# Layer 1's subset tables looked up by one float32 product in place of two float32r parts

## The chip, the core and the metric

The kernel runs on one NeuronCore of a Trainium2 chip. The metric is device time in microseconds (us) of one execution; three timed runs are summed up by their median. Beside them stands one profiled execution, from which every duration is taken. Engines are named as in the profile: PE is TensorE's matmuls, PEld its weight loads, DVE VectorE, ACT ScalarE, POOL GpSimd, SP the queue that issues most transfers.

## What is computed

Four graph layers run one after the other on 16 graphs of 1024 nodes with 128 features each; each layer's output is added to its input and normalised. The change touches layer 1 alone:

```python
def _L1_gnn_ref(x, adj, W, b):
    W1, W2 = (W[:d], W[d:])
    p = jnp.einsum('bnd,do->bno', x, W1 - W2)
    q = jnp.einsum('bnd,do->bno', x, W2)
    pre = p[:, :, None, :] + q[:, None, :, :] + b
    h = jax.nn.relu(pre) * adj[..., None]
    return jnp.max(h, axis=2)
```

For each node this is the maximum of `q` over the node's neighbours, plus `p`, cut at zero. Layer 0 is attention over the adjacency, layer 2 a sum over neighbours and two dense products. Layer 3 first thins the adjacency row by row, which is a long serial chain, and then runs three graph convolutions with batch norms.

## The kernel before, in words

**Maximum by tables.** The 1024 possible neighbours of a graph are cut into groups of six (`GS`). For each group there is a table of 64 rows: entry s is the largest `q` among the neighbours whose bit is set in s. `tables_of` builds these tables on DVE with features on partitions (`sub`). Which subset a node has is counted on PE: `count` multiplies a constant of plus and minus ones (`lit`) with the adjacency (`AT`), ACT turns the result into a one-hot column (`hot`), and a product of table and one-hot column picks the right entry (`look_up`). Two groups stand in one step: one in the upper 64 partitions, the other in the lower 64. DVE then takes the running maximum (`best`) of the 2 x 512 results.

**Slots.** One step of twelve neighbours is a slot; a graph has 86 (`NP`), and all 16 graphs 1376. Each slot has two halves of 512 nodes. In each half the program issues: the look-up of slot s into a two-bank buffer `pg` (two such buffers); pieces of layers 0 and 2 and of layer 3's thinning that a planner finds due; the count for slot s + 2; and, on DVE, the maximum over `pg`. Every second slot `table` transposes the next two steps' tables from `sub` (two transposes into `pt`) and ACT copies them out. The order in this loop on PE, ACT, DVE and POOL is written out by the program (`tc.manual_schedule`). The planner's costs and due times are constants in the code and the change does not touch them. Layer 3's thinning runs mainly on POOL and DVE beside the slots, from the generator `dilation`. After the loop come the rest of that thinning and layer 3's convolutions (`edges`, `convolve`, `sage`, `second`, `summed`).

**How a table gets its precision before.** [...] So the table is split into a high and a low float32r part. `table` writes `high`, the table cast to float32r, by ACT. `low_part`, called in the first half of every odd slot, adds `-high` to the bank that still holds the table (a product with `less`, minus the identity) and ACT casts what is left to `low`. `look_up` then multiplies `high` and `low` with `hot`, which is float32r too, and adds them in PSUM:

```python
for k, part in enumerate(tables[s - at]):
    for a in range(2):
        rows = slice(64 * a, 64 * a + 64)
        nc.tensor.matmul(pg[:, a], part[rows, at * P:(at + 1) * P], hots[s][rows, halves[h]],
                         start=(k == 0), stop=(k == 1))
```

For each half that is four products of 64 x 128 by 64 x 512: upper rows high, lower rows high, upper rows low, lower rows low. `pm` and `pt` share two banks (tag "subset"), `pg` has four.

Lines that matter: L106 `less`, L746 `hot`, L748 and L749 the count, L760 and L763 the table, L768 and L770 the low part, L779 the look-up, L831 the maximum, L286 other float32 products of 512 columns (`product_of`), used here to read what a float32 product takes.

Of the kernel before, what the change touches and what calls it, by code (L numbers as in the profile page):

```python
# [29 lines left out]
F32 = mybir.dt.float32  # L30
F32R = mybir.dt.float32r
# [8 lines left out]
B, N, D, H2 = 16, 1024, 128, 256  # L40
P = 128
# [30 lines left out]
def tile_graph_layers(ctx: ExitStack, tc, a, out):  # L72
    nc = tc.nc
    x, adj, adjT = a["x"], a["adj"], a["adjT"]
    halves = (slice(0, 512), slice(512, 1024))

    consts = ctx.enter_context(tc.tile_pool(name="consts", bufs=1))
# [13 lines left out]
    ident = consts.tile([P, P], F32, name="ident")  # L91
# [10 lines left out]
    nc.vector.memset(mhalf, -0.5)  # L102
    lit = consts.tile([CH, PC, P], F8, name="lit")
    nc.gpsimd.dma_start(out=lit, in_=a["lit"])
    less = consts.tile([P, P], F32R, name="less")
    nc.vector.tensor_scalar_mul(less, ident, -1.0)  # L106
    one_less = consts.tile([P, 1], F32, name="one_less")
    nc.sync.dma_start(out=one_less, in_=a["one_less"])

# [126 lines left out]
    def layers_012():  # L236
# [7 lines left out]
        w2 = right.enter_context(tc.tile_pool(name="w2", bufs=1, side="right"))  # L244
# [206 lines left out]
        def tables_of(b):  # L451

            if b:
                yield ask("V", 0, urgent=True, after=("tables", b - 1))
            for g0 in range(0, NP, TG):
                n_g = 2 * min(TG, NP - g0)
                yield ask("V", 0.01, same=True, urgent=True, after=("q", b))
                made.append((b, g0))
                yield ask("V", 0.1, same=True, urgent=True, after=("used", *made[-3]) if len(made) > 2 else None)
                qg = qs[b].rearrange("o (g s) -> o g s", s=GS)  # L460
                subs[b, g0] = w2.tile([P, TG, P], F32, name="sub", bufs=2)
                sub = subs[b, g0].rearrange("o t (a s) -> o (t a) s", a=2)
                nc.vector.memset(sub[:, :n_g, 0:1], LOWEST)
                for k in range(GS):
                    n = 1 << k
                    yield ask("V", 0.06 + n * n_g / 960, same=(n < 8), urgent=True)
                    nc.vector.tensor_max(sub[:, :n_g, n:2 * n], sub[:, :n_g, 0:n],  # L467
                                         qg[:, 2 * g0:2 * g0 + n_g, k:k + 1].to_broadcast([P, n_g, n]))
                happened["sub", b, g0] = now
            happened["tables", b] = now  # L470
# [214 lines left out]
        def load_x(b):  # L685
            X[b] = apool.tile([P, T, D], F32, name="X", bufs=3)
            nc.sync.dma_start(out=X[b], in_=x[b].rearrange("(t p) d -> p t d", p=P))
# [5 lines left out]
        def load_columns(at):  # L693
            b, c = divmod(at, T + 1)
            if b < B:
                rows = min(CH, N - c * CH)
                t = AT[at] = apool.tile([CH, N], F8, name="AT", bufs=4)
                if rows < CH:
                    nc.gpsimd.memset(t, 0.0)
                nc.gpsimd.dma_start(out=t[:rows], in_=adjT[b, c * CH:c * CH + rows])  # L700

        An, AT, subs, qs, ps, values, exps, bests, hots, tables = ({} for _ in range(10))
# [8 lines left out]
        def start(stream, first=False):  # L711
            pending[stream] = [next(stream, None), -9]
            streams.insert(0 if first else len(streams), stream)
# [27 lines left out]
        def count(s, h):  # L741

            b, g = divmod(s, NP)
            c, r = divmod(g, PC)
            if h == 0:
                hots[s] = w2.tile([P, N], F32R, name="hot", bufs=3)  # L746
            pm = psum.tile([P, 512], F32, tag="subset", name="pm", bufs=2)
            nc.tensor.matmul(pm, lit[:, r, :], AT[b * (T + 1) + c][:, halves[h]], start=True, stop=True)  # L748
            nc.scalar.activation(hots[s][:, halves[h]], pm, AF.Relu, bias=one_less)  # L749

        def table(s):

            b, g = divmod(s, NP)
            g0 = g - g % TG
            assert ("sub", b, g0) in happened, (s, [(x.__name__, pending[x]) for x in streams], room)
            pt = psum.tile([P, 512], F32, tag="subset", name="pt", bufs=2)[:, :2 * P]
            if g + 2 - g0 == min(TG, NP - g0):
                happened["used", b, g0] = now
            for k in range(2):
                nc.tensor.matmul(pt[:, k * P:(k + 1) * P], subs[b, g0][:, g - g0 + k, :], ident, is_transpose=True,  # L760
                                 start=(k == 0), stop=(k == 1))
            high = w2.tile([P, 2 * P], F32R, name="high", bufs=2)
            nc.scalar.copy(high, pt)  # L763
            tables[s] = pt, high

        def low_part(s):
            pt, high = tables[s]
            nc.tensor.matmul(pt, less, high, start=False, stop=True, skip_group_check=True)  # L768
            low = w2.tile([P, 2 * P], F32R, name="low", bufs=2)
            nc.scalar.copy(low, pt)  # L770
            tables[s] = high, low

        def look_up(s, h, pg):

            at = s % 2
            for k, part in enumerate(tables[s - at]):
                for a in range(2):
                    rows = slice(64 * a, 64 * a + 64)
                    nc.tensor.matmul(pg[:, a], part[rows, at * P:(at + 1) * P], hots[s][rows, halves[h]],  # L779
                                     start=(k == 0), stop=(k == 1))  # L780

        def finish(b):

            if b:
                best = bests.pop(b - 1)
                nc.vector.tensor_max(best[:, 0], best[:, 0], best[:, 1])
                nc.vector.tensor_add(ps[b - 1], best[:, 0], ps[b - 1])
            if b < B:
                bests[b] = w4.tile([P, 2, N], F32, name="best")

        def slot(s, last):

            nonlocal now, due, wants_bank
            now = s
            b, g = divmod(s, NP)
            if s >= 0 and g == 0:
                finish(b)
                if b + 1 < B:
                    start(tables_of(b + 1), True)
                    load_x(b + 1)  # L800
                    start(attend(b + 1))
                    start(scores(b + 1))
                if b:
                    start(rest(b - 1))
            if s >= 0 and g % PC == 0:
                load_columns(b * (T + 1) + g // PC + 2)
            for h in range(2):
                now = s + 0.5 * h
                for e in ROOM:
                    room[e] = min(room[e] + ROOM[e] / 2, ROOM[e])  # L810
                if s >= 0:
                    pg = psum.tile([P, 2, 512], F32, tag="wide", name="pg", bufs=2)
                    look_up(s, h, pg)
                advance(("PE",))
                advance(("A", "V", "Pool"))
                if s >= 0 and due <= now and not (wants_bank and taken >= 2 and given.get(taken - 2, 1e9) > now):
                    after, cost, wants_bank = next(dilate, (B * NP, 0, False))
                    due += after
                    room["V"] -= cost
                if h == 0 and s % 2 and s + 1 < last:  # L820
                    low_part(s + 1)
                if s + 2 < last:
                    count(s + 2, h)
                    if h and s % 2 == 0:
                        table(s + 2)
                if s >= 0:
                    own = bests[b][:, :, halves[h]]
                    if g == 0:
                        nc.vector.tensor_copy(own, pg)
                    else:  # L830
                        nc.vector.tensor_max(own, own, pg)  # L831
            if s >= 0:
                hots.pop(s)
# [19 lines left out]
        with tc.manual_schedule(engines={mybir.EngineType.PE, mybir.EngineType.Activation, mybir.EngineType.DVE,  # L853
                                         mybir.EngineType.Pool}):
            for s in range(-2, B * NP):
                slot(s, B * NP)
            finish(B)
        assert not streams, streams
        last = rest(B - 1)
# [68 lines left out]
    def load_share(b):  # L928
        part = sb.tile([P, N], F32, name="share")
        nc.sync.dma_start(out=part, in_=share[b].partition_broadcast(P))  # L930
        return part
# [132 lines left out]
    with ExitStack() as es:  # L1064
        layers_012()
# [8 lines left out]
    for b in range(B):  # L1074
        x0 = sb.tile([P, T, D], F32, name="h", bufs=2)
        nc.sync.dma_start(out=x0, in_=x3[b])
        part = load_share(b)
# [3 lines left out]
        if b + 1 < B:  # L1081
            start = len(nc.cur_bb.bb.instructions)
# [16 lines left out]
    for b in range(B):  # L1099
        near = ep.tile([P, T, N], F8, name="near", bufs=2)  # L1100
        nc.sync.dma_start(out=near, in_=kept[b])
        part = load_share(b)
# [72 lines left out]
```

## Time and profile before

| | us |
|---|---|
| runs | 6573.1, 6579.31, 6581.36 |
| median | 6579.31 |
| span of the profiled execution | 6568.2 |
| slots, from the first to the last look-up | 131.3 to 5278.8 |

Over the whole span, busy time and instructions by engine, and the span in 40 slices (each digit a busy share in tenths, PEclk the granted clock of TensorE in tenths):

```profile
PE 5661.4 (86%) x27177; PEld 2873.0 (44%) x27306; DVE 5317.8 (81%) x8130; ACT 3780.8 (58%) x6665; POOL 3794.2 (58%) x11157
...
PE   6989898989898989899989898888888768877998
PEld 3434344444343444444444444444443335555654
DVE  3999899999899999999999999999998844444445
ACT  4656566666666666666666666666665533333755
POOL 2675767676767776767677776767676611110113
PEclk8989899999898989898989998999898878888999
```

The first 32 slices are the slots: PE and DVE both nearly full. The last eight are layer 3. The groups of the look-up and of the table, by line (busy us, mean ns of one, then idle time of the engine before them and who ended it):

```profile
L749 ACT ACTIVATE hot<-pm,one_less 128x512 fp32r<-128x512 f32 x2752 | 1882.1, 688 | 1118.0 <-PE pm L748 1107.3
L779 PE MATMUL pg<-hot,high 64*128 64x512 f32 x5504 | 1471.9, 532 | 468.0 <-DVE best L831 426.2
L779 PE MATMUL pg<-hot,low 64*128 64x512 f32 x5504 | 1166.7, 420 | 0.0
...
L770 ACT CAST low<-pt 128x256 fp32r<-128x256 f32 x688 | 255.5, 371 | 393.7 <-PE pt L768 389.3
...
L768 PE MATMUL pt<-high,less 128*128 128x256 f32 x688 | 300.9, 437 | 66.3 <-ACT high L763 58.7
L760 PE MATMUL pt<-ident,sub 128*128 128x128 f32 x1376 | 292.8, 297 | 24.5 <-ACT hot L749 22.0
```

[...] records overlap, and the sum of durations is above the time that the engine was held; a step from one start to the next tells more. "64*128 64x512" is a product whose weights have 64 rows and 128 columns and whose moving operand has 64 rows and 512 columns.

### The profile page before, as it was taken

How to read it: one execution, taken by the hardware profiler on the slowest of the kernel's cores; microseconds unless marked ns; L12 is line 12 of the kernel's file. 1: busy time of each engine (PE TensorE's matmuls, PEld its weight loads, DVE VectorE, ACT ScalarE, POOL GpSimd, SP SyncE). 2: the span in 40 equal slices, each digit the busy share in tenths (PEclk: the TensorE clock that was granted, in tenths of full speed). 3: DMA queues.
4: the chain of work that ended last, by engine and by line, in shares of the span. 5: the costliest groups of instructions: out<-in, count | busy, mean ns of one | idle time of the engine just before them, and what ended most of it. 6: DMA issues, size and time to landing. Idle time of an engine off the chain costs nothing. (4 is left out here: it accounts for less than half of the span.)

```text
span 6568.2 us, 85836 instructions
## 1 busy us (share of the span) xinstructions
PE 5661.4 (86%) x27177; PEld 2873.0 (44%) x27306; DVE 5317.8 (81%) x8130; ACT 3780.8 (58%) x6665; POOL 3794.2 (58%) x11157
## 2 busy tenths in 40 slices
PE   6989898989898989899989898888888768877998
PEld 3434344444343444444444444444443335555654
DVE  3999899999899999999999999999998844444445
ACT  4656566666666666666666666666665533333755
POOL 2675767676767776767677776767676611110113
PEclk8989899999898989898989998999898878888999
DMA  5121212121212121212121212121110056564555
GB/s 38 13 28 23 31 23 36 21 28 26 28 26 29 24 30 27 27 27 28 26 27 27 30 26 33 23 31 27 27 26 12 14 80 125 110 119 106 199 170 183
DMA packets 478380, 317.00 MB, mean 48 GB/s; under 512 B 301162, under 2 KB 429668, under 8 KB 473828
## 3 DMA queue, kind: packets, MB, share of 16 engines
q0 software_dynamic: 105648, 84.20, 14.9%
q1 hardware_dynamic: 367600, 226.13, 11.9%
q8 instruction: 213, 3.49, 0.2%
q10 hardware_dynamic: 4676, 1.19, 0.1%
q14 instruction: 243, 1.99, 0.1%
HBM read 412.71 MB, written 117.18 MB: 81 GB/s over the span
## 5 line engine op out<-in xcount | busy, mean ns | idle before, releaser
L831 DVE TENSOR_TENSOR best<-best,pg 128x1024 f32<-128x1024 f32 x2720 | 3234.4, 1211 | 298.4 <-PE pg L779 289.4
L749 ACT ACTIVATE hot<-pm,one_less 128x512 fp32r<-128x512 f32 x2752 | 1882.1, 688 | 1118.0 <-PE pm L748 1107.3
L779 PE MATMUL pg<-hot,high 64*128 64x512 f32 x5504 | 1471.9, 532 | 468.0 <-DVE best L831 426.2
L779 PE MATMUL pg<-hot,low 64*128 64x512 f32 x5504 | 1166.7, 420 | 0.0
L748 PE MATMUL pm<-AT,lit 120*128 120x512 fp8e4 x2752 | 1135.9, 413 | 17.9 <-ACT hot L749 10.1
L779 PEld LDWEIGHTS pg<-hot,high 64*128 64x128 f32 x5504 | 545.7, 195 | 1271.7 <-DVE best L831 801.5
L616 POOL TENSOR_SCALAR sc<-low_counts,half_mask,rest 16x1 f32<-16x1 f32 x992 | 426.5, 430 | 403.9 <-DVE rest L603 310.1
L779 PEld LDWEIGHTS pg<-hot,low 64*128 64x128 f32 x5504 | 570.2, 204 | 0.0
L748 PEld LDWEIGHTS <-lit 120*128 120x128 fp8e4 x2752 | 273.7, 99 | 618.7 <-issue 556.1
L621 POOL TENSOR_SCALAR sc<-sc 16x1 f32<-16x1 f32 x992 | 425.5, 429 | 105.0
L770 ACT CAST low<-pt 128x256 fp32r<-128x256 f32 x688 | 255.5, 371 | 393.7 <-PE pt L768 389.3
L618 POOL TENSOR_SCALAR sc<-sc 16x1 f32<-16x1 f32 x992 | 351.6, 354 | 107.7
L980 POOL TENSOR_TENSOR length<-length,mhalf 128x8 f32<-128x8 f32 x48 | 78.9, 1644 | 572.2 <-DVE length L979 572.2
L624 POOL TENSOR_SCALAR last_rank<-V,sc 16x31 f32<-16x31 bf16 (+30 forms) x992 | 384.7, 388 | 0.0
L623 POOL TENSOR_SCALAR hit<-V,sc 16x31 bf16<-16x31 bf16 (+30 forms) x992 | 372.7, 376 | 0.0
L768 PE MATMUL pt<-high,less 128*128 128x256 f32 x688 | 300.9, 437 | 66.3 <-ACT high L763 58.7
L467 DVE TENSOR_TENSOR sub<-sub,q 128x24 f32<-128x24 f32 (+11 forms) x768 | 306.5, 400 | 24.6 <-ACT q L289 10.5
L937 ACT CAST m<-near 128x1024 fp32r<-128x1024 fp8e4 x256 | 253.4, 1044 | 113.1 <-DVE near L906 59.4
L619 POOL TENSOR_SCALAR sc<-sc 16x1 f32<-16x1 f32 x992 | 269.9, 272 | 83.4
L760 PE MATMUL pt<-ident,sub 128*128 128x128 f32 x1376 | 292.8, 297 | 24.5 <-ACT hot L749 22.0
L626 POOL TENSOR_TENSOR low_counts<-low_counts,hit 16x31 f32<-16x31 f32 (+30 forms) x992 | 264.6, 267 | 77.7
L377 PE MATMUL pav<-v,eT 128*128 128x128 f32 x2048 | 307.6, 296 | 1.9 <-ACT eT L370 1.9
(258 smaller groups left out, 9431.7 us busy)
## 6 DMA issues: line engine op xcount, KB each, us to landing
removed<-gone SPq DMA_DIRECT2D x128, 256.0 KB
An<-in_adj_dram POOLq DMA_DIRECT2D x16, 1024.0 KB, 14.8
E<-in_adj_dram POOLq DMA_DIRECT2D x128, 128.0 KB, 6.8
gone_all<-removed POOLq DMA_DIRECT2D x64, 256.0 KB, 12.1
near<-in_adjT_dram POOLq DMA_DIRECT2D x16, 1024.0 KB, 17.3
kept<-near SPq DMA_DIRECT2D x16, 1024.0 KB
share<-share SPq DMA_DIRECT2D x32, 512.0 KB
hidden<-r SPq DMA_DIRECT2D x32, 512.0 KB
```

The lines of the kernel that those rows point to most:

```text
L377: nc.tensor.matmul(pav, eT[:, c, :], values[b][:, c, :], start=(c == 0), stop=(c == T - 1))
L467: nc.vector.tensor_max(sub[:, :n_g, n:2 * n], sub[:, :n_g, 0:n], qg[:, 2 * g0:2 * g0 + n_g, k:k + 1].to_broadcast([P, n_g, n]))
L616: gp.tensor_scalar(half, mine, half_mask[:, m], rest[:, n:n + 1], op0=ALU.mult, op1=ALU.add)
L618: gp.tensor_scalar(sf, half, 5.5, sf, op0=ALU.is_gt, op1=ALU.mult)
L621: gp.tensor_scalar(to, at, sf, none, op0=ALU.subtract, op1=ALU.subtract)
L623: gp.tensor_scalar(hit[:, n, n + 1:], V[:, n, n + 1:], at, None, op0=ALU.is_equal)
L624: gp.tensor_scalar(last[:, n + 1:], V[:, n, n + 1:], to, None, op0=ALU.is_le)
L748: nc.tensor.matmul(pm, lit[:, r, :], AT[b * (T + 1) + c][:, halves[h]], start=True, stop=True)
L749: nc.scalar.activation(hots[s][:, halves[h]], pm, AF.Relu, bias=one_less)
L768: nc.tensor.matmul(pt, less, high, start=False, stop=True, skip_group_check=True)
L779: nc.tensor.matmul(pg[:, a], part[rows, at * P:(at + 1) * P], hots[s][rows, halves[h]], start=(k == 0), stop=(k == 1))
L831: nc.vector.tensor_max(own, own, pg)
```

## The change

The table is no longer split. `table` copies it out of PSUM once, as float32; `low_part` and `less` are gone; `hot` is float32; and `look_up` makes one float32 product for each half of the rows:

```diff
-    less = consts.tile([P, P], F32R, name="less")
-    nc.vector.tensor_scalar_mul(less, ident, -1.0)
...
-                hots[s] = w2.tile([P, N], F32R, name="hot", bufs=3)
+                hots[s] = w2.tile([P, N], F32, name="hot", bufs=3)
...
-            high = w2.tile([P, 2 * P], F32R, name="high", bufs=2)
-            nc.scalar.copy(high, pt)
-            tables[s] = pt, high
-
-        def low_part(s):
-            pt, high = tables[s]
-            nc.tensor.matmul(pt, less, high, start=False, stop=True, skip_group_check=True)
-            low = w2.tile([P, 2 * P], F32R, name="low", bufs=2)
-            nc.scalar.copy(low, pt)
-            tables[s] = high, low
+            tables[s] = w2.tile([P, 2 * P], F32, name="table", bufs=2)
+            nc.scalar.copy(tables[s], pt)
...
-            for k, part in enumerate(tables[s - at]):
-                for a in range(2):
-                    rows = slice(64 * a, 64 * a + 64)
-                    nc.tensor.matmul(pg[:, a], part[rows, at * P:(at + 1) * P], hots[s][rows, halves[h]],
-                                     start=(k == 0), stop=(k == 1))
+            for a in range(2):
+                rows = slice(64 * a, 64 * a + 64)
+                nc.tensor.matmul(pg[:, a], tables[s - at][rows, at * P:(at + 1) * P], hots[s][rows, halves[h]],
+                                 start=True, stop=True)
...
-                if h == 0 and s % 2 and s + 1 < last:
-                    low_part(s + 1)
```

For each half of a slot there are two float32 products where there were four float32r products, and every second slot has one product and one ACT cast less.

## The prediction

> **What bounds the kernel now.** I read, in this order, the page's slices, the granted clock, the busy times of the slot loop, the groups by line, TensorE's own timeline in a dense stretch, and TensorE's waits. Busy times by stretch, the slot loop (first to last `pg` product) in the first line, columns busy microseconds of PE, PEld, DVE, ACT, POOL, then granted clock, DMA share and GB/s:
>
> ```profile
> 131.00:5279.00 5148.00, 4529.59 (x22015) 2168.15 (x22141) 4704.24 (x6944) 3168.41 (x5820) 3563.30 (x10742) 0.91 0.19 26
> ```
>
> The loop has 16 x 86 = 1376 slots: 5148 / 1376 = 3.741 us a slot, 78% of the span. DVE is busy for 91% of it (3.42 us a slot), PE for 88% (idle 618 us, 0.45 us a slot), ACT for 62%. Two engines are near their limit, DVE nearer. Who waits, TensorE's waits and then the groups:
>
> ```profile
> PE pg L779 <- DVE best L831: 426.2, 415, 12.8
> PE pt L768 <- ACT high L763: 57.9, 231, 1.6
> ...
> PE pg L779 <- DVE sub L463: 32.8, 37, 3.2
> ...
> L831 DVE TENSOR_TENSOR best<-best,pg 128x1024 f32<-128x1024 f32 x2720 | 3234.4, 1211 | 298.4 <-PE pg L779 289.4
> ```
>
> TensorE waits for DVE (426 us) more than DVE for TensorE (289 us): a balance leaning to DVE. How long a product really holds TensorE is not its duration but the step from its start to the next start. Timeline of PE, full clock (start, length, line, tile):
>
> ```profile
> 1991.18 0.39 PE L748 MATMUL pm<-AT,lit 120*128 120x512 fp8e4 x1
> 1991.51 0.50 PE L779 MATMUL pg<-hot,high 64*128 64x512 f32 x2
> 1991.84 0.40 PE L779 MATMUL pg<-hot,low 64*128 64x512 f32 x2
> 1992.17 1.13 PE L286 MATMUL pp<-xT,w_L_gnn_W 128*128 128x512 f32 x2
> 1993.13 0.38 PE L748 MATMUL pm<-AT,lit 120*128 120x512 fp8e4 x1
> ...
> 2008.30 0.39 PE L768 MATMUL pt<-high,less 128*128 128x256 f32 x1
> 2008.52 0.39 PE L748 MATMUL pm<-AT,lit 120*128 120x512 fp8e4 x1
> ```
>
> The reader is to see three things. The two 64-row look-ups of one part (x2) take 0.33 us together, not 0.33 each: single records start 3 ns apart, so the upper and lower 64 rows of the array run side by side. One half of a slot spends 0.33 us on `high` and 0.33 on `low`. And one true float32 product of 512 columns (`pp`) is two records and holds TensorE for 0.96 us: in single records the second starts 0.53 us after the first (0.105 of it a weight load that nothing covers, 0.428 the stream), and the next product 0.428 later. An engine view of what TensorE would need without waits: in 300 to 5100 us of the trace I replaced each step from start to start by the 20th percentile, at full clock, of steps between the same two kinds of product. The sum is 3831 of 4800 us: 2.985 us a slot. The rest of the 3.741 is 0.45 of waits and about 0.31 of half clock (the records grant half speed in 807 of those 4800 us).
>
> [...] a 512-column step is 0.217 to 0.227 us[...] and 2 x 0.428 for `pp`. [...] 3 ns between the partners, and the step out of a `pg` pair is 0.325 us, 0.109 more than the stream. [...] The trace has no counterexample, but also no place that tests it with a free row group behind a busy one; the prediction rests on this. [...] the records show 1.0 and 0.5 only.
>
> **The change, part by part, per slot of two halves.**
>
> 1. Removed on TensorE: the product with `less`, 688 times 0.22 us (timeline, 2008.30 to 2008.52), half a time a slot: -0.11 us. With it goes the wait for `high` (58 us in all, in the idle time below).
> 2. Removed on ACT: 688 `low` casts of 0.371 us, 255 us. ACT is 62% busy and waits 1107 us for `pm`, so this is hidden. The float32 copy `table` replaces the cast `high` (0.366 us), and `hot` becomes float32 with the same 128x512 size; the nearest float32 row, `z` at 687 ns, equals today's 688. Nothing. On DVE one start-up instruction goes. DVE, POOL keep their order; ACT's and SP's differ only in a few places near the loop's end, SP by no added transfer. Nothing.
> 3. The look-up. Today two fp32r parts, each a pair: steps 0.334 + 0.325 = 0.659 us a half. New: one float32 product per row half, hence four records, in program order upper 1, upper 2, lower 1, lower 2, since the records of one product stand together (as in `pp`). Upper 2 needs the rows of upper 1. Lower 1 needs other rows, but stands behind upper 2, so in strict order it starts with it; lower 2 comes after lower 1. Three stages instead of two pairs: 0.533 (first stage with its weight load) + 0.428 + 0.428 and 0.109[...] = 1.498 us. Added: 0.839 a half, 1.68 a slot.
>
> The trace shows no float32 product on 64 rows, so its cost has two bounds: 2 stages if the row halves overlap fully (0.533 + 0.537 = 1.070 us a half, +0.411), and 4 if they don't overlap (1.926 us, +1.267). Below nothing I exclude by `pp`: two records of 0.428 each is what a product costs. I take 3. If a weight load of the lower rows isn't pulled ahead, 0.105 a half is added.
>
> Sum: TensorE's need 2.985 - 0.11 + 1.68 = 4.55 us a slot against DVE's unchanged 3.42. TensorE becomes the bound: what lay in its 0.45 us of idle is far too little to take 1.57. What stays of its idle: the waits on DVE came from DVE being 91% busy; at 3.42 of about 4.75 it is 72% busy, `pg` has two buffers, and I keep a third of today's waits, 0.15 us. Half clock shrinks with the idle: I keep 0.05. Slot 4.75 us, loop 1376 x 4.75 = 6536 us, 1388 more than 5148. What comes before and after the loop (1420 us) has no edit in it. Profiled execution: 6568 + 1388 = 7956. The median of the runs, 6579.3, is 11 above the profiled span; I add these: 7967, say 7965 us.
>
> **The rivals.**
>
> *No overlap* (four stages): 2.985 - 0.11 + 2 x 1.267 = 5.41, with 0.13 idle 5.54 us a slot, loop 7623, time about 9050. For it: nothing shows float32 passes side by side. Against: fp32r, the same four-byte operands, runs side by side.
>
> *Full overlap* (two stages): 2.985 - 0.11 + 0.82 = 3.69, close to DVE's 3.42, so both limit each other as now and most of the idle stays (0.45 in all): 4.14 us, loop 5697, time about 7140. For it: both row groups are free when the four stand ready. Against: it needs lower 1 to overtake upper 2.
>
> *Not slower*: the float32 look-up fits into TensorE's idle. Place: L779; price: with 0.45 idle and 0.11 freed, 0.56 us a slot; it decides if a half's look-up stays under 0.659 + 0.28 = 0.94 us. If it took only one pair's 0.334, DVE would bind alone and at most about half of its 289 us of waiting for `pg` would go: some 6430 us. Against it: even full overlap gives 1.07. That the change doesn't do what it says would look like this: `pg` with the fp32r step.
>
> **How the numbers follow.** Chances: three stages 0.78, four 0.10, two 0.09, not slower 0.03. The likeliest one's own range: no waits and no half clock, 4.55 x 1376 = 6261, time about 7690; with uncovered weight loads (0.21) and today's half clock (0.31) beside 0.15 of waits, 5.22 us, would be 8620, of which I take most, 8450. That holds perhaps 0.75; to hold 0.8 the range reaches down to 7150, into the two-stage case. A measurement of this kernel tells about 0.2% (13 us) from no change. Slower by more than that: 0.97; faster 0.02; the same 0.01.
>
> **What would show it.** `less`, `low` gone; `pg` 11008 records in one group, the step of a half 1.5 us at full clock, with the second and third record starting together about 0.53 us after the first. DVE's waits for `pg` rise from 289 to over 1000 us, TensorE's for `best` fall below 200, DVE's busy share falls to about 72% in the loop, granted clock there above 0.95. Wrong if all four records come as two pairs or in a single row, if DVE still ends most waits, or if the time outside the loop moves by more than a few microseconds.

## The result and the profile after

| us | before | after |
|---|---|---|
| median | 6578.89 (4 runs) | 6924.4 (4 runs, 6922.93 to 6931.54) |
| span of the profiled execution | 6568.2 | 6924.0 |
| start of the first to end of the last look-up | 131.3 to 5279.5 | 129.8 to 5639.3 |

The changed kernel takes 1.0527 times the time of before, 95% interval 1.0512 to 1.0542: slower, by 346 us, where 1386 were forecast. All of it is in the slot loop: that is 361 us longer (5509.5 against 5148.2), and what follows the loop takes 1285 us where it took 1289. A slot takes 4.004 us, not 3.741 and not the forecast 4.75.

The slot loop of the changed kernel by busy time (PE, PEld, DVE, ACT, POOL, then granted clock, DMA share, GB/s):

```profile
130.00:5639.00 5509.00, 5201.27 (x21329) 1941.35 (x21452) 4780.29 (x6948) 2987.59 (x5133) 3571.74 (x10742) 0.98 0.18 24
```

PE has gone from 88 to 94% busy, DVE from 91 to 87%; DVE's busy time itself is 76 us longer in a loop 361 us longer. The clock in the loop rose from 0.91 to 0.98. Its slices, and then the groups of the look-up (busy us, mean ns, idle time before them and who ended it):

```profile
PE   6989999999999999999999999999998877778998
PEld 3323333333333333333333333333333234555654
DVE  3888888888888888888898888888888864444445
...
PEclk8999999999999999999999999999999988888999
```

```profile
L818 DVE TENSOR_TENSOR best<-best,pg 128x1024 f32<-128x1024 f32 x2720 | 3285.7, 1214 | 616.4 <-PE pg L768 608.5
L768 PE MATMUL pg<-hot,table 64*128 64x512 f32 x11008 | 3167.8, 653 | 252.0 <-DVE best L818 224.5
```

The lead has changed sides: DVE waits 608 us for the look-up where it waited 289, TensorE 225 us for DVE where it waited 426. How the look-up itself runs, from TensorE's timeline (start, length, line, tile):

```profile
2006.40 1.13 PE L768 MATMUL pg<-hot,table 64*128 64x512 f32 x4
2007.46 0.39 PE L746 MATMUL pm<-AT,lit 120*128 120x512 fp8e4 x1
2007.82 1.13 PE L768 MATMUL pg<-hot,table 64*128 64x512 f32 x4
2008.88 0.70 PE L327 MATMUL psc<-kT,qT 128*128 128x512 f32 x1
```

Four records hold TensorE for 1.06 us (2006.40 to 2007.46). Their single starts over the loop, medians: 0, 7 ns, 533 ns, 540 ns. The look-up runs in two stages, each a pair, and not in three.

With the count of the prediction (every step from start to start replaced by the 20th percentile, at full clock, of steps between the same kinds) a slot of each profiled execution splits as follows. "Rest" is what is left of the slot after need and idle. In the rows with half clock at 4% or more most of it is what half clock costs (in the kernel before, the step from one pair of look-ups to the next is 0.333 us at full clock and 0.589 at half), and the share of the counted stretch (from 300 us to some 180 us before the loop's end) at half clock stands beside it.

| kernel | slot us | need | PE idle | rest | half clock |
|---|---|---|---|---|---|
| before | 3.741 | 2.99 | 0.44 | 0.31 | 17% |
| after | 4.004 | 3.67 | 0.21 | 0.12 | 4% |
| one fp32r part, split kept (e3) | 3.716 | 2.61 | 0.59 | 0.52 | 37% |
| one fp32r part, no split (e5) | 3.682 | 2.45 | 0.67 | 0.56 | 38% |
| float32 look-up, split kept (e4) | 4.064 | 3.73 | 0.19 | 0.14 | 3% |
| float32, all 128 rows twice (e8) | 4.852 | 4.76 | 0.07 | 0.02 | 0% |
| float32, same 64 rows twice (e2) | 5.874 | 5.41 | 0.02 | 0.44 | 14% |

### The profile page after: what moved, and what is told of

Its sections match the earlier page's. It is cut to its first block, busy times and chain, and to the rows that moved or that the text cites. A ratio compares the mean times of both kernels' runs of the same rounds, so it can differ in the third digit from the quotient of the medians.

```text
span 6924.0 us, 83158 instructions
## 1 busy us (share of the span) xinstructions
PE 6330.7 (91%) x26489; PEld 2644.6 (38%) x26618; DVE 5391.8 (78%) x8129; ACT 3600.5 (52%) x5977; POOL 3803.3 (55%) x11157
## 3 DMA queue, kind: packets, MB, share of 16 engines
q14 instruction: 233, 1.91, 0.1%
## 5 line engine op out<-in xcount | busy, mean ns | idle before, releaser
L818 DVE TENSOR_TENSOR best<-best,pg 128x1024 f32<-128x1024 f32 x2720 | 3285.7, 1214 | 616.4 <-PE pg L768 608.5
L768 PE MATMUL pg<-hot,table 64*128 64x512 f32 x11008 | 3167.8, 653 | 252.0 <-DVE best L818 224.5
L747 ACT ACTIVATE hot<-pm,one_less 128x512 f32<-128x512 f32 x2752 | 1887.2, 687 | 1943.8 <-PE pm L746 1935.8
L768 PEld LDWEIGHTS pg<-hot,table 64*128 64x128 f32 x11008 | 842.2, 187 | 1039.8 <-issue 499.5
L746 PE MATMUL pm<-AT,lit 120*128 120x512 fp8e4 x2752 | 1074.7, 391 | 13.4 <-ACT hot L747 7.3
L619 POOL TENSOR_SCALAR sc<-sc 16x1 f32<-16x1 f32 x992 | 420.1, 424 | 104.8
L616 POOL TENSOR_SCALAR sc<-sc 16x1 f32<-16x1 f32 x992 | 365.6, 369 | 107.5
L375 PEld LDWEIGHTS pav<-v,eT 128*128 128x128 f32 x2048 | 254.2, 196 | 186.6 <-issue 91.0
L617 POOL TENSOR_SCALAR sc<-sc 16x1 f32<-16x1 f32 x992 | 276.0, 278 | 83.2
L615 POOL TENSOR_SCALAR sc<-sc 16x1 f32<-16x1 f32 x992 | 255.9, 258 | 86.7
L937 PE MATMUL pagg<-m,high 128*128 128x512 f32 x768 | 277.2, 432 | 13.2 <-ACT high L930 13.2
L327 PE MATMUL psc<-kT,qT 128*128 128x512 f32 x512 | 288.2, 645 | 0.2
```

What stands on the lines that cost most here:

```text
L375: nc.tensor.matmul(pav, eT[:, c, :], values[b][:, c, :], start=(c == 0), stop=(c == T - 1))
L616: gp.tensor_scalar(sf, half, 5.5, sf, op0=ALU.is_gt, op1=ALU.mult)
L619: gp.tensor_scalar(to, at, sf, none, op0=ALU.subtract, op1=ALU.subtract)
L768: nc.tensor.matmul(pg[:, a], tables[s - at][rows, at * P:(at + 1) * P], hots[s][rows, halves[h]], start=True, stop=True)
L937: nc.tensor.matmul(pa[:, s], piece[:, c, :], m[c][:, s], start=(c == 0 and k == 0), stop=(c == T - 1 and k == 1))
```

## The experiments

**e1: does a product for free rows overtake one that waits?** The kernel before with its four fp32r products in another order.

```diff
-            for k, part in enumerate(tables[s - at]):
-                for a in range(2):
-                    rows = slice(64 * a, 64 * a + 64)
+            for a in range(2):
+                rows = slice(64 * a, 64 * a + 64)
+                for k, part in enumerate(tables[s - at]):
```

> The kernel before with its four fp32r products in the order upper high, upper low, lower high, lower low instead of upper high, lower high, upper low, lower low; nothing else. Theory A (a product for free rows overtakes one that waits for its own rows): the records still start as two pairs, the second of a pair 6 to 7 ns behind the first instead of 3, the step of a half stays 0.66 us, time within 0.3% of before (6580 us). Theory B (strict program order; the two stages of the changed kernel come from something special to float32): three stages, 0.334 + 0.217 + 0.325 = 0.876 us a half, TensorE's need 2.99 + 0.43 = 3.42 us a slot, time 6750 to 6850 us.

Measured: 6570.24 us, 1.0006 times before (0.9999 to 1.0013). The built program's TensorE list around a look-up reads

```
L748 Matmult pm<-AT,lit
L779 Matmult pg<-hot,high
L779 Matmult pg<-hot,low
L779 Matmult pg<-hot,high
L779 Matmult pg<-hot,low
```

and TensorE's timeline of this run shows another order:

```profile
2006.63 0.39 PE L748 MATMUL pm<-AT,lit 120*128 120x512 fp8e4 x1
2006.95 0.50 PE L779 MATMUL pg<-hot,high 64*128 64x512 f32 x2
2007.29 0.40 PE L779 MATMUL pg<-hot,low 64*128 64x512 f32 x2
2007.62 0.39 PE L748 MATMUL pm<-AT,lit 120*128 120x512 fp8e4 x1
```

Both `high` records start before the first `low`: the lower rows' `high` has passed the upper rows' `low`, which stands ahead of it. The second record of a pair starts 7 ns after the first here, as in the changed kernel, and 3 ns in the kernel before, where nothing is passed. In the built program of the changed kernel the four records of every look-up stand as upper, upper, lower, lower, so its two pairs (starts at 0, 7, 533 and 540 ns) are the same passing. Theory B falls; the order of the look-ups is worth nothing.

**e2: what the overlap saves.** The changed kernel with both look-ups on the upper 64 rows.

```diff
-                rows = slice(64 * a, 64 * a + 64)
+                rows = slice(0, 64)
```

> The changed kernel with both look-ups of a half taken from the upper 64 rows (the lower group's table is left out of the maximum). The same four float32 records, none with rows of its own. If the overlap of the two row halves is what kept the change cheap: the four records start one after the other, 0.533 + 3 x 0.428 + 0.109 = 1.93 us a half, need 3.67 + 1.71 = 5.38 us a slot, with 0.1 to 0.2 of idle 5.5 to 5.6, time 8950 to 9100 us. If float32 records of 64 rows are simply shorter than 0.43: well below 8500 us.

Measured: 9487.32 us, 1.4457 times before (1.4427 to 1.4486). Single starts 0, 533, 963, 1392 ns, the next product at 1.91 us:

```profile
2005.34 1.98 PE L768 MATMUL pg<-hot,table 64*128 64x512 f32 x4
2007.25 1.12 PE L284 MATMUL pp<-xT,w_L_gnn_W 128*128 128x512 f32 x2
```

The step was expected at 1.93 us, the need, measured as 5.41, at 5.38. So float32 records of 64 rows are as long as those of 128 (0.430 us from the second to the third start, 0.428 for `pp`), and only the overlap makes the look-up cheap: without it the kernel takes some 2560 us more. Of the 1.87 us that a slot is longer, 1.74 are need. The time is 390 us above the range given, and the idle is not the reason: it is 0.02 us a slot. The missing time is at half clock, in 14% of the stretch. The next run is about that.

**e8: half an array and the clock.** The same four records over all 128 rows.

```diff
-                rows = slice(64 * a, 64 * a + 64)
+                rows = slice(0, P)
```

> The changed kernel with both look-ups of a half taken over all 128 rows (each result then adds the two groups' entries: the maximum over neighbours is not computed). Four float32 records in a row as in the run on the same 64 rows, but no change of tiling and a full array. Steps of a half 4 x 0.43, first weight load hidden at most places: need about 5.0 us a slot. If half of the array standing empty is what had the clock granted at half for 14% of the loop there, with TensorE idle for under 1%: the share of half clock falls below 3%, slot 5.0 to 5.15, time 8300 to 8500 us. If it is due to something else: half clock stays near 14%, time above 8700 us.

Measured: 8089.68 us, 1.2326 times before (1.2301 to 1.2351); the slot loops of e2 and of this run:

```profile
130.00:8212.00 8082.00, 8048.07 (x21454) 3103.02 (x21453) 4878.51 (x6948) 3025.78 (x5132) 3479.58 (x10742) 0.92 0.12 17
```

```profile
131.00:6808.00 6677.00, 6585.62 (x21330) 3217.82 (x21454) 4831.96 (x6951) 3018.65 (x5133) 3530.24 (x10742) 1.00 0.14 20
```

TensorE is 99% busy in both, and the clock is 0.92 in the first, 1.00 in the second: half clock fell from 14% of the counted stretch to 0.2%. In that stretch half clock began 13 times in e2, each time after 3.4 us in which TensorE was busy for 41 to 74%, and 4 times here, after 3.4 us with 29 to 41%; in the kernel before it began 76 times, after 3.4 us with at most 67%. What differs is how long it stays: 3.4 us each time here, 17 to 475 us in e2, although TensorE was busy for 96 to 100% of that time. One of the cases of e2, the gap and the half clock after it (columns as above: after the length of the stretch PE's busy time, and the clock third from the end):

```profile
3096.80:3100.20 3.40, 1.58 (x6) 0.78 (x6) 3.26 (x8) 0.95 (x2) 0.00 (x0) 0.99 0.00 0
3100.20:3209.40 109.20, 109.20 (x172) 38.40 (x171) 46.60 (x57) 25.07 (x39) 57.14 (x172) 0.50 0.18 20
```

The work at the end of these stretches differs from the rest. Cut into pieces of 3.4 us, each half clock in e2 ended with a piece in which products of 120 or 128 rows held TensorE for 65% of the time or more (13 of 13); of the 359 other pieces in which it was at least 97% busy, 346 had less. So in e2 the full clock came back behind products of 120 or 128 rows. That the number of rows decides it is not shown: e2 and e8 also differ in the changes between 64 and 128 rows and in the weight loads.

The time is below the range given because four records hold TensorE for 1.72 us: the first step is 0.43 us and not 0.53, the last 0.43 and not 0.52. The need is 4.76, not 5.0.

**e3: does TensorE's need count before the change?** The kernel before without the product over `low`.

```diff
-            for k, part in enumerate(tables[s - at]):
+            for k, part in enumerate(tables[s - at][:1]):
...
-                                     start=(k == 0), stop=(k == 1))
+                                     start=(k == 0), stop=True)
```

> The kernel before with the look-up of the low part left out of the product (the low part is still made). TensorE's need falls by one pair, 2 x 0.334 = 0.67, to 2.32 us a slot, below DVE's 3.42. If TensorE's need and DVE's share in the time of a slot: 6300 to 6450 us. If DVE alone set the time before: no change beyond 0.5%. DVE can't go below 1376 x 3.42 = 4706 us of loop, 6130 us in all.

Measured: 6529.98 us, 0.9945 times before (0.993 to 0.9961). Between the two theories, much nearer to the second. Its need fell by 0.38 us a slot, not 0.67, since the one pair left holds TensorE for 0.43 us, not for half of the 0.66 that two pairs took. Of the 0.38, idle took 0.15 and the rest, mostly half clock (17% of the stretch before, 37% here), 0.21; the slot became 0.025 us shorter. DVE is busy for 92% of its loop. Before the change TensorE had next to nothing to give.

**e4: what the split cost.** The split made as before, but one float32 product over the bits of `high`.

```diff
-            for k, part in enumerate(tables[s - at]):
-                for a in range(2):
-                    rows = slice(64 * a, 64 * a + 64)
-                    nc.tensor.matmul(pg[:, a], part[rows, at * P:(at + 1) * P], hots[s][rows, halves[h]],
-                                     start=(k == 0), stop=(k == 1))
+            for a in range(2):
+                rows = slice(64 * a, 64 * a + 64)
+                nc.tensor.matmul(pg[:, a], tables[s - at][0].bitcast(F32)[rows, at * P:(at + 1) * P],
+                                 hots[s].bitcast(F32)[rows, halves[h]], start=True, stop=True)
```

> The float32 look-up alone: the kernel before with its split into high and low kept (product with minus the identity, both casts), but looked up as one float32 product over the high table's bits (the low part is left out of the result). If the removed chain was worth what its steps add up to, 0.11 us a slot of TensorE: 150 us above the changed kernel's 6924, 7050 to 7090 us. If the chain's removal was hidden: 6924 within 0.3%. More than 7090 would mean that its wait for ACT counts too.

Measured: 7011.34 us, 1.0683 times before (1.0667 to 1.0699), 87 us above the changed kernel by the medians; by the loops of the two profiles it is 83 us, 0.060 us a slot. Against the kernel before, which was 12 us faster in this set of runs, it is 99 us, 0.072 a slot. So the chain's removal was not hidden, but worth a half to two thirds of the 0.11 counted for it. The steps show a part of the reason: in the kernel before, 206 of the 332 `less` products that follow a product of 128 rows start within 40 ns of it. In 26 of these places that product is the second record of `pp`, and the count behind the two starts 0.551 us after it; without `less` between them it starts after 0.429 (medians): 0.12 us more, not 0.22. How much of the chain this makes in all stays open.

**e5: the split gone, fp32r kept.** Table and one-hot column of the changed kernel as float32r.

```diff
-                hots[s] = w2.tile([P, N], F32, name="hot", bufs=3)
+                hots[s] = w2.tile([P, N], F32R, name="hot", bufs=3)
...
-            tables[s] = w2.tile([P, 2 * P], F32, name="table", bufs=2)
+            tables[s] = w2.tile([P, 2 * P], F32R, name="table", bufs=2)
```

> The changed kernel with table and one-hot column as float32r: one pair of fp32r products a half, no split (the low part of the table is left out). Need of TensorE about 2.61 - 0.06 = 2.55 us a slot, far below DVE's 3.42. If DVE sets the time there: no faster than the run that left only the low look-up out, 6510 to 6535 us, TensorE idle 0.6 us a slot or more. If TensorE's need still counts in part: 6480 to 6510 us.

Measured: 6473.26 us, 0.9865 times before (0.9846 to 0.9884): the fastest of all runs, and faster than both theories' ranges, by 7 us for the second. TensorE's need does count in part, but in small part: it is 0.54 us a slot below that of the kernel before, and the slot is 0.06 us shorter. The run leaves the tables' low part out of the maximum, so it is less precise and no repair of the change. Against e3 the product with `less` and a cast are gone; which of the two made it 57 us faster than e3 the runs don't separate. DVE waits 184 us for the look-up in place of 266:

```profile
PE pg L768 <- DVE best L818: 678.3, 727, 12.1
DVE best L818 <- PE pg L768: 184.2, 302, 11.5
```

**e6: is TensorE the bound after the change, and does a change of tiling cost?** The count on 64 rows, as the look-up is.

```diff
-    lit = consts.tile([CH, PC, P], F8, name="lit")
-    nc.gpsimd.dma_start(out=lit, in_=a["lit"])
+    lit = consts.tile([64 + CH // 2, PC // 2, P], BF, name="lit")
+    for i in range(2):
+        nc.gpsimd.dma_start(out=lit[64 * i:64 * i + CH // 2], in_=a["lit"][CH // 2 * i:CH // 2 * (i + 1), PC // 2 * i:PC // 2 * (i + 1)])
...
-                t = AT[at] = apool.tile([CH, N], F8, name="AT", bufs=4)
+                t = AT[at] = apool.tile([64 + CH // 2, N], BF, name="AT", bufs=3)
...
-            nc.tensor.matmul(pm, lit[:, r, :], AT[b * (T + 1) + c][:, halves[h]], start=True, stop=True)
+            rows = slice(64 * (2 * r // PC), 64 * (2 * r // PC) + CH // 2)
+            nc.tensor.matmul(pm, lit[rows, r % (PC // 2), :], AT[b * (T + 1) + c][rows, halves[h]], start=True, stop=True)
```

> The changed kernel with the count's product laid on 64 rows (60 of them filled) in bf16, in place of 120 rows of fp8, so that the array isn't switched between 64 and 128 rows between count and look-up; two transfers for each adjacency tile in place of one, three buffers for four. If a switch costs the 0.105 us on each side that the steps show and TensorE sets the time of the changed kernel: up to 0.2 us less need a half where a count stands next to a look-up on both sides (about half of them), 0.1 on the others, 0.2 to 0.4 us a slot in all, loop 150 to 400 us shorter with what idle comes back, 6600 to 6780 us. If TensorE does not set it, or the switch costs nothing: 6924 within 0.5%.

Measured: 6809.42 us, 1.0372 times before (1.0355 to 1.039), 115 us below the changed kernel by the medians, 103 us by the distances to the kernel before. That is just outside the range for the first theory and three times the band of the second. TensorE's relief shortens the loop, so TensorE does set the time after the change, at least in part; the relief is smaller than counted. A change between 64 and 128 rows does cost: the look-up holds TensorE for 0.96 us where a product of 64 or 60 rows follows and for 1.06 us where one of 128 rows follows (20th percentiles at full clock). But the run also lets count and look-up overlap, and its gain can't be split between the two: in 937 of the 2062 places where a look-up record is the next to start after a count, it starts within 20 ns, as here:

```profile
2003.43 0.39 PE L751 MATMUL pm<-AT,lit 60*128 60x512 bf16 x1
2003.44 1.24 PE L773 MATMUL pg<-hot,table 64*128 64x512 f32 x4
```

## Why the prediction was wrong, point by point

**What bounds the kernel before.** Right, and more so than it was put: a balance leaning to DVE. e3 shows that TensorE's idle was not a reserve that turns into time when it is given more room.

**Sign and bound after.** Right: slower, with TensorE ahead of DVE in the waits. The size of the waits was not: DVE's for `pg` 608 us, not over 1000; TensorE's for `best` 225, not below 200; DVE 87% busy, not 72%. All three go with the next point.

**The step that failed** is the third part, "Lower 1 needs other rows, but stands behind upper 2, so in strict order it starts with it". It does not wait. The prediction rested there on the assumption of strict program order, and said that no place in the trace tested it. e1 tests it, and the measurement decides: across row groups a product passes one that waits for its own rows, and starts 7 ns after the first. So the look-up took two stages, 0.533 + 0.527 = 1.060 us a half, not three of 1.498 in all. The difference of 0.438 is 0.88 us a slot, or some 1200 us of loop: more than the 1041 us by which the forecast was too high, because the 0.20 us a slot kept for idle and half clock came out at 0.33. That half clock shrinks with the idle was an estimate: from before to after both fell, idle from 0.44 to 0.21 us and half clock from 17 to 4%, but e2 has 0.02 us of idle and 14% of half clock.

**The bounds for that step** were right. The lower one, 1.070 us for full overlap, was measured as 1.060; the upper one, 1.926 for no overlap, as 1.91 in e2. The 0.105 us of weight load in them stands in the trace of before: the first load of `pp` starts 2 ns ahead of its record and the second record follows 0.533 us after the first, while in the 12 places where at full clock the load leads by 0.106 us or more it follows after 0.429 to 0.433. The 0.109 us was put down, without support, to the change from 64 to 128 rows behind a pair: in the trace of before the step between two pairs without such a change, 0.334 us, is no shorter than the 0.325 out of a pair. In e6 the look-up's step is 0.10 us shorter where no such change follows. What fills that time is not shown. The rival with full overlap was the true case, given 0.09. Its need of 3.69 was measured as 3.67; its time of 7140 (its own terms add up to 7128) was 216 us too high, mostly because it kept 0.45 us a slot for idle and half clock together. They were 0.33: TensorE waits less for DVE (225 us, not 426), and the clock in the loop is 0.98, not 0.91. The prediction had also named two pairs as a sign that it was wrong, and that sign came.

**What was to cost nothing.** ACT's busy time in the loop fell by 181 us, from 62 to 54%. That its casts cost nothing is not shown: no run takes them away alone, and e4's 0.06 to 0.07 us a slot hold the product with `less` and the casts together. The `hot` column as float32: 687 ns against 688. Outside the loop: 4 us.

**The removed chain**: mis-sized, 0.06 to 0.07 us a slot where 0.11 were counted (e4).

So the loop's 361 us come from 0.68 us a slot more need, of which idle gave back 0.23 and the rest 0.19. About three fifths of the added work went into time that TensorE lost before.

## What to carry to other kernels

Two true float32 products on 64 rows each, one on either half of the rows, took two steps here (0.53 us each) and not three or four, because TensorE let a product for free rows pass one that waited for its own (it started 7 ns after the first); before counting stages, reorder such products in a run of the old kernel and look at the starts. TensorE had idle time because DVE leaned to being the bound, and work added on it was still hidden only in part: 0.42 of 0.68 us a slot. Where a step of the forecast rests on an assumption that the trace doesn't test, its bounds should carry more of the chance than the assumption.

## What the runs showed of the hardware that was not expected

Matmuls of different row groups pass each other: the second started 7 ns after the first with a waiting product between them in the program (e1), 3 ns without one (before). A change from products of 64 rows to one of 128 cost about 0.10 us (e6, 0.96 against 1.06). Once the granted clock had fallen after a gap, it stayed at half for 17 to 475 us with TensorE 96 to 100% busy where its look-ups used 64 rows one after the other (e2), and for 3.4 us where they used 128 (e8). And the half-clock share rose from 17 to 37% when one pair of look-ups a half was taken away (e3): the need fell by 0.38 us a slot, and the rest of the slot grew by 0.21.
